# Products with zeros added to the scans' sums where TensorE's pacing clock is behind VectorE's

## The chip, the core and the metric

The kernel runs on one core of one Trainium2 chip. A core has TensorE (PE, with its weight loads shown as PEld), VectorE (DVE), ScalarE (ACT), GpSimd (POOL) and SyncE (SP), which here only issues DMAs. The metric is the device time in microseconds of one execution; the profile is one further execution, with its own time.

## The reference

Four images of 32x32 tokens and 256 channels pass four layers. Cut to what matters, with the scans written out:

```python
# layer 0, for each image: norm, projection, depthwise conv, GELU -> x [L, 512]; then a selective scan
dt = softplus(dt_raw @ w_dt + dt_bias)            # L = 1024 steps, 512 channels
h  = exp(dt[:, :, None] * A) * h + (dt * x)[:, :, None] * B[:, None, :]   # 64 states
y  = einsum('bdn,bn->bd', h, C)
# layer 1: grouped 3x3 convolution between two 1x1 ones, residual
# layer 2: masked attention with 8 heads over 1024 tokens, then 8 experts with the top 2 of a router
# layer 3: a gated selective scan with 16 states, then 8 experts with the top 2 of a router
```

Each image has one scan of layer 0 and one of layer 3. An image's later layers need all of its earlier ones.

## The kernel before

A scan step handles 128 rows (channel times state) over all 1024 positions. A scan of layer 0 has 256 such steps, one of layer 3 has 64; the eight scans make 1280, in the order of the list `SCANS` ((layer, image)). For step k the generator `scans` issues, in this order:

- `load(k + 4)`: DMAs on SP's queue that spread a row of dt over partitions, into one of five `dA` buffers;
- `first(k + 1)`: two bf16 products on PE that spread the inputs, into one of two `ps_rep` buffers in PSUM. The buffer is free when the scan two steps earlier is done;
- `decay(k + 2)`: ACT's exponential of `dA`;
- DVE's product of `ps_rep(k)` with the row B (1.21 us), and after a yield its `tensor_tensor_scan` (2.29 us), then POOL's product of `h` with the row C (2.37 us);
- every second step `pair(k - 2)`: four fp32 products with the table `collect` on PE, which sum two `h` tiles over the states into `ps_y`, each on its own 32 of the 128 output partitions.

`ps_y` has one buffer. A sum stays open for 16 pairs (layer 0) or 4 pairs (layer 3). Its first pair starts the accumulation, its last one closes it, ACT copies it to `yo` and SP stores it. There are 64 such sums.

All other work is "side work": generators for the fronts of images 1 to 3 (`front`), the middle of each image (`middle`: end of layer 0, layer 1, attention, experts, start of layer 3) and its end (`last`), in the order of `STAGES`. A stage starts when the scan that it names is done. Every engine executes its instructions in the order in which the program issues them, so the mixing of side work into the scans is fixed when the program is built, by the loop in `run`. That loop keeps a modelled clock for each engine. A wrapper, `Metered`, adds a fixed price to an engine's clock for every instruction issued: `matmul_us` charges 0.46 ns a column for bf16 products (0.2355 us for 512 columns), four times that for fp32, and less for narrow tiles. After each half step of a scan, every clock is first raised to at least `LAG` (4.0 us) behind DVE's; then up to `TICKS` (2) pieces of side work are issued, while no engine's clock is ahead of DVE's by more than `LEAD` (0.0):

```python
LEAD, LAG, TICKS = 0.0, 4.0, 2
```

Where a scan needs results that side work has not produced (`need`), side work is issued without pacing until it has, and all clocks are set to the latest. After the last scan step the remaining side work follows, and then the end of image 3. The first image's front comes ahead of all scans.

## Time and profile before

| | |
|---|---|
| time, median of 3 runs (lowest, highest) | 7049.76 us (7038.85, 7057.48) |
| time of the profiled execution | 7061.6 us |
| span of the profiled execution | 7059.5 us |
| mean granted clock of TensorE | 0.812 |
| busy: PE, DVE, ACT, POOL | 5383.6, 5212.0, 3462.1, 3650.0 us |
| PE instructions in the profile (products, weight loads) | 20516, 20516 |
| `ps_rep` products of DVE, its scans: count, mean | 1280, 1213 ns; 1280, 2285 ns |
| `ps_y` records on PE, mean | 5120, about 750 ns |

The span is from the first to the last instruction. A row of 40 digits shows the span in 40 slices of 176 us; a digit is the busy share in tenths, 9 being 90% or more, and for `PEclk` it is the granted clock of TensorE in tenths of full speed. An fp32 product appears as two records. Where the kernel records operations through the wrapper, all have line 120 (`Metered`), so groups are told apart by the names of their tiles. A line of the waits reads: engine, tile and line that waited, what it waited for, then the sum in us, the number of waits and the longest one.

### The profile page before, as it was taken

What the parts mean: (1) busy time and instruction counts of PE and PEld (TensorE: products, weight loads), DVE (VectorE), ACT (ScalarE), POOL (GpSimd) and SP (SyncE); (2) the same over time, 40 slices, a digit from 0 to 9 for tenths busy, and PEclk for the clock granted to TensorE, in tenths of its full rate; (3) what the DMA queues carried; (4) which work ended last, traced back from release to release, by engine and by line L of the source; (5) the groups of instructions that cost most, each with busy time, mean ns of one, the idle gap of its engine ahead of it and who ended that gap; (6) DMA issues with size and microseconds to landing.
All of it is one profiled execution on the core that took longest, in us unless ns stands there. A gap on an engine that the chain in (4) does not pass through costs nothing. (4 is left out here: it accounts for less than half of the span.)

```text
span 7059.5 us, 66331 instructions
## 1 busy us (share of the span) xinstructions
PE 5383.6 (76%) x20516; PEld 2218.2 (31%) x20516; DVE 5212.0 (74%) x4477; ACT 3462.1 (49%) x4162; POOL 3650.0 (52%) x1801
## 2 busy tenths in 40 slices
PE   7185876578898567879779668898698677957979
PEld 3020221032253022224235332242254322513556
DVE  2787898887898986789889877898899831247511
ACT  3254666244477324447658434577386332244511
POOL 1288677664556754555766554556656520045300
PEclk9585876578888567979879778898698889877989
DMA  2355666654456565446656654456666620135421
GB/s 82 77 139 158 161 178 167 169 143 120 115 143 176 160 172 136 119 116 171 176 151 164 178 144 120 115 143 178 165 168 165 162 70 6 44 107 152 113 63 33
DMA packets 395053, 939.03 MB, mean 133 GB/s; under 512 B 83268, under 2 KB 165776, under 8 KB 393040
## 3 DMA queue, kind: packets, MB, share of 16 engines
q1 hardware_dynamic: 392512, 932.10, 49.0%
q8 instruction: 172, 2.82, 0.2%
q0 software_dynamic: 2128, 2.13, 0.2%
q14 instruction: 241, 1.97, 0.1%
HBM read 844.17 MB, written 93.95 MB: 133 GB/s over the span
## 5 line engine op out<-in xcount | busy, mean ns | idle before, releaser
L120 POOL TENSOR_TENSOR h<-h,rows 128x1024 f32<-128x1024 f32 x1280 | 3024.2, 2365 | 2138.8 <-DVE h L120 1756.0
L120 DVE TENSOR_TENSOR_SCAN h<-dA,ps_rep 128x1024 f32<-128x1024 f32 x1280 | 2924.7, 2285 | 228.0 <-issue 94.6
L120 DVE TENSOR_TENSOR ps_rep<-ps_rep,rows 128x1024 f32<-128x1024 f32 x1280 | 1553.0, 1213 | 338.7 <-PE ps_rep L120 317.0
L120 ACT ACTIVATE dA<-dA,A_L_conv_A_log 128x1024 f32<-128x1024 f32 x1024 | 1152.8, 1145 | 695.2 <-DMA dA<-dt 600.6
L120 PE MATMUL ps_rep<-S,spread_L_conv_A_log 96*128 96x512 bf16 x2048 | 763.2, 463 | 899.6 <-DVE h L120 731.7
L120 PE MATMUL ps_y<-h,collect_L_conv_A_log 128*32 128x512 f32 x4096 | 750.2, 755 | 91.1 <-POOL h L120 91.1
L120 ACT ACT_TABLE_LOAD x494 | 633.8, 1283 | 174.7 <-DMA dA<-dt 115.0
L120 PEld LDWEIGHTS <-spread_L_conv_A_log 96*128 96x128 bf16 x2048 | 164.5, 103 | 1661.3 <-DVE h L120 1213.5
L120 PE MATMUL ps_h<-xTm,we 128*128 128x512 f32 x1280 | 605.2, 609 | 7.6 <-ACT h_m L120 6.6
L120 PE MATMUL ps_e<-we,h_m 128*128 128x256 f32 x2560 | 587.9, 381 | 10.1 <-ACT h_m L120 10.1
L120 ACT ACTIVATE p<-ps_sc 128x512 f32<-128x512 f32 x512 | 277.9, 595 | 587.2 <-PE ps_sc L120 573.8
L120 ACT ACTIVATE dA<-dA,A_L_attn_A_log 128x1024 f32<-128x1024 f32 x256 | 293.6, 1148 | 490.1 <-DMA dA<-dt 456.4
L120 PEld LDWEIGHTS ps_e<-we,h_m 128*128 128x128 f32 x2560 | 481.8, 190 | 140.6 <-issue 46.0
L120 PE MATMUL ps_at<-p,v 128*32 128x512 f32 x1024 | 363.6, 627 | 63.1 <-ACT p L120 55.7
L120 PE MATMUL ps_rep<-S,spread_L_attn_A_log 96*128 96x512 bf16 x512 | 191.4, 464 | 280.8 <-DVE h L120 239.2
L120 ACT ACTIVATE h_m<-ps_h,cols 128x512 f32<-128x512 f32 x320 | 216.5, 687 | 302.2 <-PE ps_h L120 299.3
L120 DVE SCALAR_TENSOR_TENSOR tb<-ps_e,cw,tb 128x256 f32<-128x256 f32 x448 | 192.6, 473 | 200.5 <-PE ps_e L120 200.5
L120 PEld LDWEIGHTS ps_h<-xTm,we 128*128 128x128 f32 x1280 | 242.4, 193 | 288.1 <-issue 236.3
L120 PE MATMUL ps_sc<-qT,kT 32*128 32x512 f32 x1024 | 300.7, 663 | 0.0
L120 PE MATMUL ps_at<-p,ones 128*32 128x512 f32 x1024 | 280.1, 627 | 0.0
L120 DVE RECIPROCAL sums<-sums 128x512 f32<-128x512 f32 x16 | 53.6, 3353 | 253.4 <-ACT sums L120 253.4
L120 PEld LDWEIGHTS ps_y<-h,collect_L_conv_A_log 128*32 128x32 f32 x4096 | 98.8, 119 | 450.4 <-issue 234.3
(406 smaller groups left out, 5703.5 us busy)
## 6 DMA issues: line engine op xcount, KB each, us to landing
dA<-dt SPq DMA_DIRECT2D x2048, 256.0 KB
dA<-dt SPq DMA_DIRECT2D x2048, 64.0 KB
we<-in_L_ffn_W_dram SPq DMA_DIRECT2D x64, 512.0 KB
parts<-parts SPq DMA_DIRECT2D x64, 384.0 KB
S<-parts SPq DMA_DIRECT2D x96, 256.0 KB
dt<-sp_r SPq DMA_DIRECT2D x64, 256.0 KB
y<-yo SPq DMA_DIRECT2D x128, 128.0 KB
y_back<-y SPq DMA_DIRECT2D x64, 256.0 KB
```

The source lines that it names most:

```text
L120: return got(*args, **kw)
```

## The change

A tile of zeros (128 x 512, bf16) is kept in SBUF. After the side work of each half step, products of this tile with itself are issued on PE as long as PE's pacing clock is more than `IDLE` (0.5 us) behind DVE's. They go to the current `ps_y` tile. While a sum is open they are added to it; between two sums they start and stop on their own, in a tile that the next sum then uses. Each goes through `Metered` like other products, and so moves PE's clock by 0.2355 us. The first pair of a sum takes the `ps_y` tile that a product with zeros may already have taken.

```diff
@@ module
 LEAD, LAG, TICKS = 0.0, 4.0, 2
+
+
+IDLE = 0.5
@@ Hybrid.__init__
+        self.zeros = const.tile([P, 512], BF16, name="zeros")
+        nc.vector.memset(self.zeros, 0.0)
@@ scans
-        y = None
+        y, open_sums = None, False
...
+        def nothing():
+
+            nonlocal y
+            if y is None:
+                y = psum.tile([P, 512], F32, tag="y", name="ps_y", bufs=1)
+            nc.tensor.matmul(
+                y, lhsT=self.zeros[:, :P], rhs=self.zeros, start=not open_sums, stop=not open_sums
+            )
+
+        self.nothing = nothing
+
         def pair(k):

-            nonlocal y
+            nonlocal y, open_sums
...
-            if i == 0:
+            if y is None:
                 y = psum.tile([P, 512], F32, tag="y", name="ps_y", bufs=1)
+            open_sums = True
...
+                y, open_sums = None, False
@@ run
                 for _ in range(TICKS):
                     if max(clock.values()) > clock["vector"] + LEAD or self.advance() is None:
                         break
+                while clock["vector"] - clock["tensor"] > IDLE:
+                    self.nothing()
```

## The prediction

> **What bounds the kernel now.** I read the page's first two parts, then the busy time by stretches, then the waits of DVE, then the order of time in two short windows. The first two parts say that no engine is busy all the time and that TensorE's clock moves:

> ```profile
> span 7059.5 us, 66331 instructions
> ...
> PE 5383.6 (76%) x20516; PEld 2218.2 (31%) x20516; DVE 5212.0 (74%) x4477; ACT 3462.1 (49%) x4162; POOL 3650.0 (52%) x1801
> ...
> PE   7185876578898567879779668898698677957979
> ...
> DVE  2787898887898986789889877898899831247511
> ...
> PEclk9585876578888567979879778898698889877989
> ```

> The clock's digit follows PE's digit: 5 where PE is half busy, 9 where it is busy throughout. The 1280 scan steps lie in slices 2 to 38; there DVE is the fullest engine except in slices 33 to 35, where scans wait for a stage. In the stretches (start:end, its length, then busy time of PE, PEld, DVE, ACT, POOL, then the clock and DMA) the second line has nothing but scan steps, the third the expert layers beside them:

> ```profile
> 317.70:1387.80 1070.10, 753.06 (x2248) 196.40 (x2248) 942.97 (x626) 575.35 (x719) 796.68 (x423) 0.70 0.61 162
> 2413.70:2471.30 57.60, 31.47 (x96) 3.71 (x96) 54.58 (x33) 18.76 (x17) 37.69 (x17) 0.50 0.57 151
> 5281.50:5344.20 62.70, 60.13 (x245) 31.36 (x244) 59.31 (x45) 52.66 (x49) 37.08 (x17) 1.00 0.58 153
> ```

> Sixteen steps take 57.6 us where nothing else runs: 3.60 us a step, of which DVE works 3.41. PE does its part at half clock and still waits. With the experts, at full clock, a step takes 3.92 us and both engines are nearly full. What DVE waits for between its first and last scan step:

> ```profile
> DVE ps_rep L120 <- PE ps_rep L120: 305.1, 201, 15.7
> DVE sums L120 <- ACT sums L120: 253.4, 16, 67.2
> DVE sp_e L120 <- ACT sp_l L120: 111.3, 7, 77.3
> ```

> The first line is the only one that a faster PE shortens directly. Laying the clock's stretches in the trace over the gaps ahead of DVE's `ps_rep` products, I find 337 us of gaps over 0.15 us (the view above names PE for 305 of them), PE busy in 256 us of that, and **108 us of it at half clock**. In all gaps of DVE in the scan phase, 1312 us, PE is busy at half clock for 286 us.

> [...] its clock is only ever 0.5 or 1.0, and its 83 stretches at half clock (2651 us) last whole multiples of 3.41 us. [...] below, two `ps_rep` products start 0.43 us before their successor, 0.215 each. [...] here sixteen `ps_e` records, each with its own 128-column load, take 3.45 us, 0.216 each, so a load hides behind such a product.[...] That products with zeros count as busy no run here shows yet.

> **The change part by part.** Counted from the instruction lists of both kernels as built: PE gets 5352 products of the zeros tile (512 columns bf16, all 128 rows of `ps_y`) and as many weight loads; DVE gets one memset at the start, costed at nothing because the weights' first DMAs are still out then, ACT ten table loads more because its order shifts, POOL and SP nothing. Of the zeros 1759 fall to steps 0 to 255, 1170 to 256 to 511, 1996 to 512 to 1183, 427 to the rest.

> *Price of the zeros.* At 0.216 us they are 1156 us of PE; at half clock 0.427 and 2285 us, the upper bound. The pair of windows gives what surrounds them:

> ```profile
> 1274.69 1.03 PE L120 MATMUL ps_rep<-S,spread_L_conv_A_log 96*128 96x512 bf16 x2 [2.56 <-DVE h L120]
> ...
> 1275.65 1.94 PE L120 MATMUL ps_y<-h,collect_L_conv_A_log 128*32 128x512 f32 x8
> ...
> 1278.29 1.03 PE L120 MATMUL ps_rep<-S,spread_L_conv_A_log 96*128 96x512 bf16 x2 [0.70 <-DVE h L120]
> ```

> ```profile
> 3705.86 0.60 PE L120 MATMUL ps_rep<-S,spread_L_conv_A_log 96*128 96x512 bf16 x2
> 3706.29 3.62 PE L120 MATMUL ps_e<-we,h_m 128*128 128x256 f32 x16
> 3709.74 0.60 PE L120 MATMUL ps_rep<-S,spread_L_conv_A_log 96*128 96x512 bf16 x2
> 3710.27 1.06 PE L120 MATMUL ps_y<-h,collect_L_conv_A_log 128*32 128x512 f32 x8
> ```

> The bracket is PE's idle time and its releaser. Two steps at half clock cost PE 1.03 + 1.94 + 1.03 = 4.0 of 7.2 us; at full clock 2 x 0.43 + 1.06 = 1.92. A bare stretch gets 177 zeros in 16 steps, 22.1 in two: 4.78 us. Together **6.70 of 7.20 us**, so DVE still sets the step, PE is 93% busy, and by the third stretch above that is enough for full clock. I therefore cost the zeros at nothing in bare stretches; the cover is DVE's step, and it is gone if a zero product takes over (7.20 - 1.92) / 22.1 = 0.239 us. Where PE is the fuller engine (the experts, attention) the pacing clock leaves no room and hardly any zeros are there: none in most expert stretches, 16 to 18 in most 16-step stretches of attention.

> *Gain.* The waits of DVE on a PE at half clock lie at the start of side work after a thin stretch: the 32 small `ps_n` products ahead of attention (waits of 12.0, 11.7 and 11.3 us), attention's first block (four of 11.8 to 15.7), the routers' `ps_lg` (two of 4.7). Full clock halves the 108 us: 54 us at most in the named waits, 143 (half of 286) with all indirect ones, 0 if every such wait has another end, as some have (the mask's DMA in attention's first block). I take 45.

> *The new wait.* After a sum is closed, the next zero product takes a new `ps_y` tile (one buffer), so it waits for ACT's copy to `yo`. In the lists 24 zeros carry a wait on ACT. In the trace the copy ends 0.65 to 6.6 us after the sum's last product, median 0.7, mean 1.5: 24 x 1.5 = 36 us on PE. Queued behind is all of PE: `ps_rep` of the next step, for which DVE waits. That product may start one step early (when the scan two steps before it has freed its buffer), so 3.60 - 0.60 = 3.0 us are free; 8 of the 64 copies exceed this, by 13 us in sum. I take 5, bounds 0 and 36.

> *Lost catching up.* PE's own waits in the scan phase (`ps_y` on POOL 119 us, `ps_at` on ACT 56, the mask's DMA 38, `raw` 37, `cw` 32, `sq` 29) were followed by idle time; now zeros follow, also at half clock just after such a wait. I take 10 us, bounds 0 and 100 (a third of those 311).

> *Order.* Since PE's pacing clock now stands at most 0.5 instead of 4.0 behind DVE's, side work is let in later: up to 86 products later at a given step, level again before most stages end. SP's, ACT's and POOL's side instructions move with it. Two places lie on the path that sets the end: 30 `ps_sc` and 16 `ps_at` products go from before the unpaced stretch (5731 to 6329 us) into it, some 17 us, and 18 expert products go behind the last scan, 16 x 0.43 + 2 x 0.86 = 8.6 us. In both the steps before are rid of the same products, and DVE was waiting for PE there, so I take 0, bounds 0 and 26. ACT's ten table loads cost 1.28 us each (mean of its row), 12.8 us; ACT is busy 49% of the span and waits for dA's DMAs over 1000 us, which hides most: I take 3, bounds 0 and 13.

> Sum: -45 + 5 + 10 + 0 + 3 = **-27 us**. Against the profiled execution, 7061.6 us (span 7059.5 and 2.1 around it), that is 7034.6; it lies 11.8 above the median of the runs, 7049.8, so the forecast is **7023**.

> **Rivals.** *PE without room becomes the bound (slower).* For it: median PE work between two `ps_rep`, summed by full-clock prices, goes from 3.0 to 3.5 us of a 3.6 us step, so a PE that is late by more than 3.0 us stays late and DVE pays. Against it: the zeros stop as soon as the pacing clock is level, and that clock charges 0.2355 for a zero that takes 0.216. Price: 100 (waits paid again) + 36 (copies) + 26 (order) + 13 (table loads) - 54 = +121 at its full size, 7171; it decides where the losses pass the gain, from 45 us on, and I expect it near half, about 7105. Its extreme, a clock that zeros do not raise, would make 13.5 us (4.0 + 22.1 x 0.427) of two bare steps and cost over 1000 us; I give that 0.02.

> *Hidden anyway (same).* The waits of DVE on PE have other ends (ACT's `sq`, the mask's DMA, the arrival of S), so the clock rises and the time stays: 7050, between -20 and +20. For it: in the longest waits PE itself waits for ACT or a DMA.

> **How the numbers follow.** About 0.3%, 21 us, is what a measurement of this kernel can tell from no change. Gain as worked out 0.44, no change 0.18, PE without room 0.38. The gain's own range is 6960 to 7029; with the rivals, leaving out the extreme and the largest losses, 6955 to 7140.

> **What would show it.** After: PEclk 9 in nearly all slices of the scan phase; zeros 0.215 to 0.22 us apart; bare steps still 3.6 us; DVE's wait on `ps_rep` down from 317 us to about 265. It is wrong if bare steps lengthen (zeros too dear), if that wait grows (no room), or if PE's wait for `yo`'s copy shows tens of us with DVE idle behind it.

## The result, and the profile after

The changed kernel takes 7096.38 us (median of four runs, 7089.97 to 7104.48) against 7051.63 for the kernel before (four runs, 7038.85 to 7057.48). The ratio is **1.0067 [1.0047, 1.0086]**: 47 us slower, between 33 and 61. The forecast was 7023. The profiled execution took 7102.03 us, at a mean granted clock of 0.931 where it was 0.812.

The page of the kernel after, first and second part and one of the costliest groups (that one ends with idle time before it and what ended most of it):

```profile
span 7100.3 us, 77000 instructions
PE 6207.2 (87%) x25868; PEld 2684.0 (38%) x25868; DVE 5245.1 (74%) x4478; ACT 3473.6 (49%) x4172; POOL 3652.5 (51%) x1801
PE   7298999989999988989989888999899887978979
DVE  2788898897798986789889877798899821247511
PEclk9599999999999998989989989999999988888989
L123 PE MATMUL ps_y<-zeros 128*128 128x512 bf16 x5352 | 1329.9, 393 | 58.4 <-ACT yo L123 35.0
```

The clock rose as announced: 9 nearly everywhere, and in the trace it is at half for 988 us where it was for 2651. The products with zeros do keep TensorE's clock up here: without them the same order has 0.814 (`order_only`, below). But look at DVE: 5212.0 us busy before, **5245.1 now**, with one instruction more, a memset. The same instructions became 33 us dearer. That is where this case turns.

A bare stretch of sixteen scan steps, by the stretches view (columns as before), and two steps in it by the order of time on PE:

```profile
2413.10:2471.00 57.90, 56.11 (x276) 20.07 (x274) 54.57 (x32) 18.84 (x17) 37.80 (x17) 1.00 0.57 150
```

```profile
2425.38 1.47 PE L123 MATMUL ps_y<-zeros 128*128 128x512 bf16 x6
2426.68 0.60 PE L123 MATMUL ps_rep<-S,spread_L_conv_A_log 96*128 96x512 bf16 x2
2427.12 2.97 PE L123 MATMUL ps_y<-zeros 128*128 128x512 bf16 x13
2430.22 0.60 PE L123 MATMUL ps_rep<-S,spread_L_conv_A_log 96*128 96x512 bf16 x2
```

The stretch is 57.90 us long, against 57.60 before, at full clock instead of half. Thirteen zeros start at 2427.12 and the `ps_rep` behind the last of them follows within 3.1 us. In the trace two zeros in a row start 216 ns apart at full clock (median of 4415 pairs) and 427 at half (of 201): the price was right, and it is hidden here. What DVE waits for over the span, first one line of the kernel before, then two of the kernel after, and what PE waits for at the zeros:

```profile
DVE ps_rep L120 <- PE ps_rep L120: 317.0, 202, 15.7
```

```profile
DVE ps_rep L123 <- PE ps_rep L123: 297.4, 230, 13.4
DVE sums L123 <- ACT sums L123: 280.3, 16, 73.9
```

```profile
PE ps_y L123 <- ACT yo L123: 35.0, 18, 8.1
```

DVE's wait for `ps_rep` fell from 317 us to 297, not to 265. That for `sums` went from 253 to 280. The copies to `yo` cost PE 35 us.

Following the start of each scan step in both traces (after less before): -23 us at step 352, about 0 at step 768, +19 at step 1192, +34 at step 1204 behind the unpaced stretch, +32 at the last step, and +41 at the end. The loss is not made in one place, and at step 768 none of it is there yet.

### The profile page after: what moved, and what is told of

It is laid out like the page before. It is cut to its first block, busy times and chain, and to the rows that moved or that the text cites. A ratio compares the mean times of both kernels' runs of the same rounds, so it can differ in the third digit from the quotient of the medians.

```text
span 7100.3 us, 77000 instructions
## 1 busy us (share of the span) xinstructions
PE 6207.2 (87%) x25868; PEld 2684.0 (38%) x25868; DVE 5245.1 (74%) x4478; ACT 3473.6 (49%) x4172; POOL 3652.5 (51%) x1801
## 5 line engine op out<-in xcount | busy, mean ns | idle before, releaser
L123 DVE TENSOR_TENSOR_SCAN h<-dA,ps_rep 128x1024 f32<-128x1024 f32 x1280 | 2924.7, 2285 | 251.1 <-issue 97.6
L123 DVE TENSOR_TENSOR ps_rep<-ps_rep,rows 128x1024 f32<-128x1024 f32 x1280 | 1553.6, 1214 | 316.5 <-PE ps_rep L123 297.4
L123 PE MATMUL ps_y<-zeros 128*128 128x512 bf16 x5352 | 1329.9, 393 | 58.4 <-ACT yo L123 35.0
L123 PE MATMUL ps_rep<-S,spread_L_conv_A_log 96*128 96x512 bf16 x2048 | 633.6, 392 | 292.5 <-DVE h L123 157.6
L123 PEld LDWEIGHTS <-zeros 128*128 128x128 bf16 x5352 | 519.2, 100 | 876.7 <-issue 334.0
L123 PE MATMUL ps_y<-h,collect_L_conv_A_log 128*32 128x512 f32 x4096 | 592.0, 620 | 57.4 <-POOL h L123 57.4
L123 PE MATMUL ps_at<-p,v 128*32 128x512 f32 x1024 | 380.8, 620 | 85.6 <-ACT p L123 80.0
```

What stands on the lines that cost most here:

```text
L123: return got(*args, **kw)
```

## The experiments

All runs of this section were timed in five rounds beside the kernel before on the same chip; ratios are to it. The change has two parts that can be done apart: PE's pacing clock no longer lags far behind DVE's, which moves side work (**order**), and products are issued (**zeros**). Instruction lists show that the order on PE apart from zeros is that of the kernel after in `order_only`, `half_zeros`, `open_only`, `order_nopool` and `after_nopool`, and that of the kernel before in `zeros_only`, `zeros_open` and `before_nopool`. The engines kept to the lists: in the trace of the kernel before, as far as tile names tell the instructions apart, all 2587 of ACT and all 364 of POOL stand in the order of the list, as do 2915 of 2917 of DVE and 11650 of 11662 of PE; the others changed places with a neighbour.

### The order alone

```diff
                 while clock["vector"] - clock["tensor"] > IDLE:
-                    self.nothing()
+                    clock["tensor"] += 0.46e-3 * 512
```

> The pacing clock of PE is raised to 0.5 us behind DVE's as in the changed kernel, but no product with zeros is issued: PE's order is that of the changed kernel without its zeros. Order theory (side work let in later is what costs: 27 us more in the unpaced stretch, 8 behind the last scan): slower than before by 45 us or more, 7095 to 7135, since the loss stays and the gain of the faster clock is gone. Room theory (PE filled with zeros has no time to catch up): within 20 us of before, 7040 to 7070.

7087.74 us, ratio **1.0045 [1.0032, 1.0057]**: +32 us (23 to 40), without one product of zeros. The time lies between the two expectations: the order costs, but less than the theory said. Two thirds of the loss is an effect that the prediction had costed at 0. And the wait that the zeros were to shorten has fallen without them, further than in the kernel after (297.4):

```profile
DVE ps_rep L123 <- PE ps_rep L123: 287.4, 216, 13.0
```

### The zeros alone

The products go past the metered wrapper and are placed by a second clock, so that side work is let in as before:

```diff
-            nc.tensor.matmul(
+            self.raw.tensor.matmul(
...
+                fill += clock["tensor"] - seen
+                clock["tensor"] = max(clock["tensor"], now - LAG)
+                seen = clock["tensor"]
...
-                while clock["vector"] - clock["tensor"] > IDLE:
+                fill = max(fill + clock["tensor"] - seen, clock["vector"] - LAG)
+                seen = clock["tensor"]
+                while clock["vector"] - fill > IDLE:
                     self.nothing()
+                    fill += 0.46e-3 * 512
```

> The zeros (5242 of them) are placed by a second clock and not charged to the pacing clock: side work keeps the order of the kernel before. Order theory: faster than before by 20 to 50 us, 7000 to 7030, the gain of the full clock without the loss. Room theory: slower by 40 us or more, 7090 to 7130.

7049.65 us, ratio **0.9988 [0.9979, 0.9998]**: 8 us faster, with 5242 products and a clock of 0.926. The order theory had the sign right and the size not: the clock rose as far as in the full change, the time hardly moved. DVE's wait for `ps_rep` even became longer:

```profile
DVE ps_rep L123 <- PE ps_rep L123: 335.3, 217, 18.1
```

### Narrower zeros, and none between the sums

`half_zeros` is the kernel after with products of 256 columns at the same places, each charged as 512 on the pacing clock. `open_only` leaves out the products between sums, which wait for the copy to `yo`, and still charges them:

```diff
-            nc.tensor.matmul(
-                y, lhsT=self.zeros[:, :P], rhs=self.zeros, start=not open_sums, stop=not open_sums
+            self.raw.tensor.matmul(
+                y[:, :256], lhsT=self.zeros[:, :P], rhs=self.zeros[:, :256], start=not open_sums, stop=not open_sums
...
                     self.nothing()
+                    clock["tensor"] += 0.46e-3 * 512
```

```diff
-            if y is None:
-                y = psum.tile([P, 512], F32, tag="y", name="ps_y", bufs=1)
+            if y is None or not open_sums:
+                self.clock["tensor"] += 0.46e-3 * 512
+                return
```

> Order, number and pacing charge of the zeros as in the changed kernel, but each product has 256 columns instead of 512, so they take about 0.108 us each and 580 us of PE less. Order theory: as the changed kernel, 7085 to 7105, if PE's clock stays up. Room theory: most of the loss goes, 7050 to 7070.

> As the changed kernel, but between two sums the pacing clock is charged and no product issued, so that no zero waits for ACT's copy of the last sum (496 zeros fewer). If that wait (35 us on PE in the trace of the changed kernel) reaches DVE: 7065 to 7080. Order theory, and room theory without this wait: 7085 to 7105.

1.0036 [1.0024, 1.0049] and 1.0043 [1.003, 1.0056]; the kernel after is at 1.0067 [1.0047, 1.0086]. Halving the zeros gives back some 22 us and leaving out the closed ones some 17, with overlapping intervals. Both end level with the order alone (1.0045), within the intervals, so the order's cost stands under both.

`zeros_open` does the same on the old order, where nothing has to be charged (the kernel is `zeros_only` with `if y is None or not open_sums: return`), and `zeros_open_half` takes 256 columns there as well.

> zeros_only without products between two sums (4733 zeros, none waits for ACT's copy). If the copy wait took back part of the clock's gain: 10 to 20 us faster than zeros_only, 7025 to 7040. If the gain itself is small: as zeros_only, 7040 to 7055.

> zeros_open (order of before, no product between sums) with products of 256 columns instead of 512. Room theory: faster than zeros_open by 5 to 15 us, 7029 to 7039, if PE's clock stays up. If room costs nothing in this order: as zeros_open, 7040 to 7050.

0.9984 [0.9977, 0.9992] with 4733 products, 11 us faster, and 0.9979 [0.997, 0.9988], 7039.95 us, 15 us faster. On this order the copies are worth 3 us and the width 4, both within the intervals. The last is the quickest version found. It beats both kernels, by less than 0.3% against the one before.

### Why the order costs: POOL's product taken away

DVE's busy time points at POOL. By the tile view (least, median and greatest duration in ns, first and last start), first the kernel before, then `order_only`: eight TENSOR_SCALARs of four elements a partition.

```profile
L120 DVE TENSOR_SCALAR lny_v<-lny_mv x8: 169/170/170, 1756.2 to 5992.0; 128x4 f32<-128x4 f32 x8
```

```profile
L123 DVE TENSOR_SCALAR lny_v<-lny_mv x8: 170/1177/1939, 1758.0 to 6021.1; 128x4 f32<-128x4 f32 x8
```

An operation that takes 0.17 us takes up to 1.94. By the order of time, one of them in `order_only`, then its twin in the kernel before, each with POOL's product beside it:

```profile
1937.99 2.34 POOL L123 TENSOR_TENSOR h<-h,rows 128x1024 f32<-128x1024 f32 x1 [4.20 <-DVE h L123]
1938.20 0.18 DVE L123 BATCH_NORM_AGGREGATE lny_mv<-lny_st 128x2 f32<-128x6 f32 x1
1938.41 1.94 DVE L123 TENSOR_SCALAR lny_v<-lny_mv 128x4 f32<-128x4 f32 x1
```

```profile
1914.12 2.36 POOL L120 TENSOR_TENSOR h<-h,rows 128x1024 f32<-128x1024 f32 x1 [5.23 <-DVE h L120]
...
1916.74 0.17 DVE L120 TENSOR_SCALAR lny_v<-lny_mv 128x4 f32<-128x4 f32 x1
```

In the first, DVE's operation starts at 1938.41 while POOL's product runs and ends at 1940.35, POOL's at 1940.33. The BATCH_NORM_AGGREGATE inside the same product is not held up (0.18 us; in the kernel before also 0.18, behind POOL's product, at 1916.52). The TENSOR_SCALAR of the kernel before starts after POOL's product has ended. Of the DVE operations in `order_only` that start while POOL's product has over 0.1 us still to run, all 16 TENSOR_SCALARs and 57 of the 60 with two inputs in SBUF take over 0.1 us longer than the shortest of their group. None of the 157 BATCH_NORM operations on SBUF tiles does, and none of the 290 (TENSOR_TENSOR, SCALAR_TENSOR_TENSOR) with an input in PSUM. In the kernel after, counted the same way, it is 16 of 16, 61 of 61, none of 158 and none of 276. So the traces show the durations and which operations are hit; by what means POOL's product holds them up they don't show.

The test leaves POOL's product with the row C out (its clock is still charged), so the sums are made of `h` alone; once with the old order, once with the new, once with the whole change:

```diff
-                nc.gpsimd.tensor_tensor(h, h, Cm, ALU.mult)
+                self.clock["gpsimd"] += 2.3e-3 * L + 0.06
```

`order_nopool` sets a loss that goes with POOL's product (its first range) against side work that ends later; `after_nopool` sets a PE without room against a price of the zeros, 15 us over `order_only`, that goes with POOL's product too (its second range).

> The kernel before with POOL's product of h and the row C left out of every scan step (its price still charged to the pacing clock, so the order of everything else is unchanged). It is the base for the next run. DVE's small operations that were stretched while POOL worked go back to their short durations: about 40 to 80 us faster than before, 6970 to 7020, under every theory.

> order_only with the same product left out. [...] (the later order puts DVE's small operations on top of POOL's product[...]): most of the 29 us between order_only and before goes with the product, so this run is 0 to 12 us slower than before_nopool. Path theory (side work ends later in the unpaced stretch and behind the last scan): the difference stays at 22 us or more.

> The changed kernel with POOL's product of h and the row C left out of every step, its price still charged. With order_nopool (6912) as base it shows what the zeros themselves do[...]. Room theory (a PE filled with zeros can't catch up): 10 to 25 us slower than order_nopool, 6922 to 6937. [...] equal to order_nopool or up to 12 faster, 6900 to 6912.

| | with POOL's product | without it |
|---|---|---|
| order of before | 1 | 6925.52 us, 0.9813 [0.98, 0.9826] |
| order of after, no zeros | 1.0045 [1.0032, 1.0057] | 6911.96 us, 0.9791 [0.9778, 0.9804] |
| whole change | 1.0067 [1.0047, 1.0086] | 6908.87 us, 0.9796 [0.9782, 0.981] |

The spans and busy times of the pages of `order_only`, `before_nopool` and `order_nopool`:

```profile
span 7084.9 us, 66321 instructions
PE 5442.2 (77%) x20516; PEld 2211.3 (31%) x20516; DVE 5237.9 (74%) x4478; ACT 3474.2 (49%) x4172; POOL 3647.5 (51%) x1801
```

```profile
span 6929.3 us, 63700 instructions
PE 5325.2 (77%) x20516; PEld 2210.2 (32%) x20516; DVE 5134.6 (74%) x4477; ACT 3460.0 (50%) x4162; POOL 620.0 (9%) x521
```

```profile
span 6911.1 us, 63701 instructions
PE 5357.6 (78%) x20516; PEld 2196.2 (32%) x20516; DVE 5134.8 (74%) x4478; ACT 3472.3 (50%) x4172; POOL 619.9 (9%) x521
```

With POOL's product the new order makes DVE 25.9 us busier (5237.9 less 5212.0), and the span grows by 25.4: in these two executions that is all of the loss on balance, since DVE's idle time, span less busy time, stays at 1847 us (its wait for `ps_rep` fell by 30 us, that for `sums` grew by 27). Without the product DVE is busier by 0.2, and the **new order is then 14 us faster** than the old one, where up to 12 us slower was expected. The two were timed side by side; the intervals of their ratios just overlap, their five times each do not. So the order is dear through POOL's product: a swing of 46 us, of which the lengthened operations are 26.

The rest is unresolved. It is idle time of DVE that the new order saves without the product (1795 to 1776 us) and not with it. But leaving the product out saves 132 us on the old order, more than the 80 expected at most, with DVE's busy time down by 77: the sums on PE also stop waiting for POOL (120.0 us at `ps_y` in the kernel before; in the page of `before_nopool` PE has 0.0 us of idle time ahead of layer 0's `ps_y` products), and the run does not part the two.

An estimate from the traces gives the lengthening itself: what DVE's operations, other than the scan steps' own product and scan, take beyond the shortest of the same group while they overlap POOL's product is 75 us before, 99 in `order_only` and 108 after. Of the 24 us between the first two, 22 are TENSOR_TENSORs, most with two inputs in SBUF; the TENSOR_SCALARs shown above are the smaller part.

`mult_half` was to confirm this from the other side: on the kernel before, side work is let in only after DVE's `ps_rep` product, up to four pieces at once, so that little of it would follow a scan.

```diff
-                for _ in range(TICKS):
+                for _ in range(0 if n % 2 else 2 * TICKS):
```

> The kernel before, but side work is let in only after the half step that ends with DVE's product, up to four pieces at once, and none after DVE's scan, where POOL's product of the same step begins. [...] fewer DVE operations fall on POOL's product, DVE's busy time falls by 10 us or more and the time by 5 to 25. Path theory: side work is let in later (up to 30 products of PE, half as much as in order_only), 10 to 20 us slower.

7246.01 us, 1.0269 [1.0254, 1.0284]: neither theory's number. DVE's busy time stayed near, at 5216.7 us. The loss is in DVE's idle time, most of it in waits for PE: that for `ps_rep` was 317.0 us and that of line 120 for `ps_e` 200.5, and now they are

```profile
DVE ps_rep L120 <- PE ps_rep L120: 393.5, 162, 23.9
DVE tb L120 <- PE ps_e L120: 250.7, 116, 10.2
```

The coarser batches of side work changed more than was meant, and the run says nothing on POOL.

### Why the clock brought so little

In `zeros_open` the prediction's largest wait, the 32 small `ps_n` products ahead of attention, looks like this on PE by the order of time, with DVE's product behind it:

```profile
4182.66 3.58 PE L123 MATMUL ps_n<-byhead,sq 128*128 128x4 f32 x16 [8.84 <-ACT sq L123]
4186.17 1.94 PE L123 MATMUL ps_y<-h,collect_L_attn_A_log 128*32 128x512 f32 x8
4188.03 3.58 PE L123 MATMUL ps_n<-byhead,sq 128*128 128x4 f32 x16
4191.47 1.01 PE L123 MATMUL ps_rep<-S,spread_L_attn_A_log 96*128 96x512 bf16 x2
```

```profile
4192.52 1.23 DVE L123 TENSOR_TENSOR ps_rep<-ps_rep,rows 128x1024 f32<-128x1024 f32 x1 [12.39 <-PE ps_rep L123]
```

PE itself waits 8.84 us for ACT's `sq`. In this time the trace has nothing on PE, no zeros either (0.00 us busy from 4178.00 to 4182.60), and the clock goes back to half just ahead of the work that was to gain (mean 1.00 from 4172 to 4178, 0.53 up to 4182.60, then 0.50): `ps_rep` takes 1.01 us there and 0.60 at full clock. By the measure of the prediction (half-clock stretches laid over the gaps ahead of DVE's `ps_rep`) PE was busy at half clock in these gaps for 108.4 us before and still for **109.3 in `zeros_open`**. Other large parts of it also come behind a wait of PE: in attention's first block, in three images, 4.9 to 6.2 us at half clock follow waits of 11 to 13 us, two of them for the mask's DMA. To see what a kept clock is worth, products of 128 columns were put ahead of the first `ps_n` of each image, where PE otherwise stands and waits for `sq`: 90 in `warm_shift`, 160 in `warm_long`.

```diff
@@ zeros_open, in front of the first ps_n products
+                for _ in range(0 if i or c else 160):
+                    self.raw.tensor.matmul(
+                        n2.rearrange("p a b -> p (a b)"), lhsT=self.zeros[:, :P], rhs=self.zeros[:, :P],
+                        start=True, stop=True,
+                    )
```

> zeros_open with 90 more products of 128 columns with zeros, into the ps_n tile, ahead of its first group of products in each image's attention: there PE waits 9 us for ACT's squares, its clock falls to half, and DVE waits about 12 us behind the ps_n products in three of four images. Theory (the gain failed because PE's own wait lets the clock fall just before the work that DVE waits for): at full clock the ps_n products take half as long, DVE's four waits shrink by 2 to 7 us each, 8 to 28 us in sum, 7016 to 7036. If it is ACT that sets these waits: as zeros_open, 7040 to 7050.

> As warm_shift, but 160 products of 128 columns ahead of the first ps_n group instead of 90: some 8.8 us at full clock, so that they reach up to the end of PE's 9 us wait. In warm_shift 90 of them took 5 us and the clock had fallen 1 to 2 us before the ps_n products in three of four images. If the half clock sets these waits, the trace shows ps_n records of 0.17 us instead of 0.376 in the first group and DVE's waits of 12 us shrink by 2 to 5 us each; the time then is 5 to 15 us below warm_shift's 7055. If the waits stay at 12 us with ps_n at full clock, it is ACT's squares that set them.

Ninety were too few: in three of four images the clock was at half again 0.9 to 2.1 us ahead of `ps_n`, the three waits stayed (13.1, 12.4, 11.8 us), and the ratio is 1.0000 [0.9992, 1.0008]. With 160, at the same place as above:

```profile
4176.95 9.10 PE L1160 MATMUL ps_n<-zeros 128*128 128x128 bf16 x160
4185.89 1.90 PE L123 MATMUL ps_n<-byhead,sq 128*128 128x4 f32 x16
4187.72 1.07 PE L123 MATMUL ps_y<-h,collect_L_attn_A_log 128*32 128x512 f32 x8
4188.71 1.95 PE L123 MATMUL ps_n<-byhead,sq 128*128 128x4 f32 x16
4190.52 0.59 PE L123 MATMUL ps_rep<-S,spread_L_attn_A_log 96*128 96x512 bf16 x2
```

```profile
4191.15 1.23 DVE L123 TENSOR_TENSOR ps_rep<-ps_rep,rows 128x1024 f32<-128x1024 f32 x1 [7.92 <-PE ps_rep L123]
```

The work runs at full clock (mean 1.00 from 4176 to 4192) and DVE's wait falls from 12.39 to 7.92 us (in the three images from 12.3, 12.4, 12.2 to 8.2, 7.9, 9.8). From the start of `ps_n` to DVE's product it is 9.86 us in `zeros_open` and 5.26 here: PE's part of this wait nearly halves with the clock up, and the rest is PE's own wait for `sq`. In the first image, which came to this point with the clock already up, the products now made a wait of 8.5 us. The ratio is 0.9993 [0.9985, 1.0001], no better than `zeros_open`. The mechanism is shown at these waits; as a remedy it brought nothing.

## Why the prediction was wrong, step by step

- **Order, taken as 0: the step that failed most, +32.** The prediction looked for products moved on PE's path to the end, and took them as made good by the steps before. They are so only in part. From step 1192 to step 1204, across the unpaced stretch, `order_only` falls back by 15 us against the kernel before and `order_nopool` by 7 against `before_nopool`; DVE's wait for `sums` in that stretch (5700 to 6330 us) went from 212.2 to 238.3 us in the kernel after. Behind the last step the two lose 8 and 7 us, near the 8.6 worked out for that place. But this alone does not make the order dear: without POOL's product it loses there too, and its waits for `sums` grow by 24 us, and it is still 14 us faster, since it is 38 us ahead at step 900. With the product it is 9 ahead there.

  What the prediction did not look at is DVE's own work. It counted "one memset at the start, costed at nothing", and so took the durations of all other instructions for fixed. In the traces they depend on what POOL does at that moment (0.17 us against up to 1.94 for the same TENSOR_SCALAR), and the moved side work lands beside POOL's product: DVE is 26 us busier with the same work.

```profile
DVE sums L120 <- ACT sums L120: 212.2, 4, 67.2
```

```profile
DVE sums L123 <- ACT sums L123: 238.3, 4, 73.9
```

The same wait over the whole spans of `before_nopool` and `order_nopool`:

```profile
DVE sums L120 <- ACT sums L120: 250.7, 16, 67.0
```

```profile
DVE sums L123 <- ACT sums L123: 274.7, 16, 67.1
```

- **Gain, taken as 45, measured as 11 (6 to 16) in `zeros_open`, with what the zeros cost there already taken off.** That PE's part of such a wait nearly halves with the clock holds (`warm_long`, from `ps_n` on: 9.86 to 5.26 us). The failed term is "Full clock halves the 108 us": 109 are still at half clock, since ahead of the largest of these waits PE stands in its own wait (8.84 us in the one shown), with no zeros in it. Of the fall of DVE's `ps_rep` wait in the kernel after, the order alone makes all (287.4 us in `order_only`). The rival "hidden anyway" named that cause, PE waiting for ACT or a DMA in the longest waits, and it describes the zeros alone.
- **New wait, taken as 5.** PE's part was right: 35 us where 36 were worked out. Its worth is 3 us on the old order (`zeros_only` against `zeros_open`) and some 17 on the new one, with overlapping intervals.
- **Lost catching up, taken as 10.** Without POOL's product the zeros cost nothing that shows on the new order (0.9796 against 0.9791, overlapping). With it they add some 15 (1.0045 to 1.0067, overlapping), of which DVE's busy time shows 7; halving them takes about as much away. How the zeros' width acts there stays open.
- **Table loads, taken as 3.** There are 504, ten more, as counted. Their price was not measured apart.
- **Price of the zeros, right:** 216 ns at full clock and 427 at half, bare stretches 57.9 us, clock at 0.93.

The rival "PE without room" forecast the sign and lay within 10 us of the result, for a reason that is not the one shown: PE had room in the bare stretches, and most of the loss comes without a single product. What the prediction would have needed was in its own trace: a DVE group with one shape and a wide spread of durations, looked up against POOL's row. One such, in the kernel before:

```profile
L120 DVE TENSOR_SCALAR lnm_v<-lnm_mv x7: 172/435/1953, 1935.9 to 6429.9; 128x8 f32<-128x8 f32 x7
```

## What to carry to other kernels

When a change shifts pacing, the moved instructions are not only a question of who comes first: check which small VectorE operations fall beside a long GpSimd one (here 0.17 us became up to 1.94 beside a product of 2.34 us), and read the spread of durations of equal instructions before taking durations as fixed. In these runs the clock stayed up for the work behind PE's own wait where products filled that wait to its end: with 160 of them it was at 1.00 in the image shown, with 90 at half again 0.9 to 2.1 us ahead of `ps_n` in three of four images. Products added elsewhere raised the mean clock here from 0.812 to 0.921 for 11 us of speed. A pacing clock that charges for filler also paces everything else: place the filler by a clock of its own.

## What the runs showed of the hardware beyond this

- Products of four columns did not bring the clock up here. In `zeros_open` PE is busy for 10.01 of the 10.40 us from 4182.6 on, by the stretches view, more than two thirds of it with `ps_n`, and the clock stays at 0.50; in the bare stretch of the kernel after, PE is busy for 56.11 of 57.90 us and the clock is at 1.00. So how busy PE's row is did not tell the clock in these two. The last line of the fence is the stretch of `zeros_open`, the one above it PE's wait:

```profile
4178.00:4182.60 4.60, 0.00 (x0) 0.00 (x0) 2.13 (x1) 2.09 (x3) 3.58 (x2) 0.53 0.57 144
4182.60:4193.00 10.40, 10.01 (x43) 7.42 (x44) 0.48 (x1) 3.39 (x5) 0.32 (x1) 0.50 0.52 143
```
